# A cross-attention block whose way in and first three blocks are issued in another order

## The chip, the cores and the metric

The kernel runs on one core of a Trainium2 chip. TensorE (PE) multiplies matrices, with weight loads of its own (PEld); VectorE (DVE), ScalarE (ACT) and GpSimd (POOL) do elementwise work; SyncE (SP) issues most transfers. Each engine works through its own instructions in order and waits at semaphores for the others. The metric is device time in microseconds (us), the lower the better. All data are float32.

## The reference

x is (16, 1024, 512), the context (16, 64, 512), the condition (16, 512). Both x and the context are layer-normed and modulated by the condition, then attended with 16 heads of 32, projected, and added to x:

```
def _ada_ln(x, c, W_ss, b_ss):
    h = (x - mu) / jnp.sqrt(var + EPS)
    ss = jax.nn.silu(c) @ W_ss + b_ss
    scale, bias = jnp.split(ss, 2, axis=-1)
    return (1.0 + scale)[:, None, :] * h + bias[:, None, :]
xq  = _ada_ln(x_q,  t_vec, Wss_q,  bss_q)
xkv = _ada_ln(x_kv, t_vec, Wss_kv, bss_kv)
q = (xq @ Wq + bq).reshape(B, Lq, nh, dh)
kv = (xkv @ Wkv + bkv).reshape(B, Lkv, 2, nh, dh)
scores = jnp.einsum('bqhd,bkhd->bhqk', q, kv[:, :, 0]) / sqrt(dh)
attn = softmax(scores)
out = jnp.einsum('bhqk,bkhd->bqhd', attn, kv[:, :, 1]).reshape(B, Lq, H)
return x_q + (out @ Wp + bp)
```

## The kernel before, in words

The 16,384 query rows are 32 blocks of 512 rows (NB = 32, two per batch element). The context is two groups of 512 rows, A (batch elements 0 to 7) and B (8 to 15); all keys and values stay on chip.

The order of all work is written out by hand: the function's last part is a list of calls, and each engine gets its instructions in the order of that list. Nothing reorders them. So what stands in a queue ahead of a waiting instruction matters as much as what it waits for.

The pieces, with their lines:

- Loads: condition (95), context A in four tiles of 256 KB (117), context modulation weights in two loads of 1 MB, scales then shifts (141), key and value weights in four halves (161), block 0 of x (119), query modulation weights (141), query weights (169), context B. They all go through SP's queue. Four small bias rows go through POOL's (150).
- Modulation rows: silu of the condition (L211 to L219), then `scale_shift_rows` (L249): 16 matmuls per half; a copy (L262), a transpose (L268) and an add of the bias (L274) bring them to one column per feature and batch element. `biases` (L227 to L230) transposes the bias rows.
- Context: statistics (`q_stats`, L286 and L287), reciprocal deviation (`rstd_of`, L295 to L310), normalising on ScalarE (`hidden`, L327), 16 transposes on PE (L384), and `modulated` (L402 on ScalarE, L404 on VectorE), which scales each batch element's 64 columns of each feature chunk by its own scale and shift, in an order of columns that is taken apart by 32s.
- Products of 512x512x512 use seven half-sized products instead of eight (`seven`, L503): product n takes a half of the weights, or a sum of halves (`column_sums`, L447 to L450, on POOL), and a half of the features or a sum (`feature_sums`, L467 to L470). Each is 8 matmuls. Results leave through `key_out`, `query_out` (ScalarE, L562, L542), `key_added`, `query_added` (VectorE, L568, L549), `value_out` and `value_added` (L582, L587); `seed` (L515) copies a partial sum into a second bank. For group A the products run 1, 2, 6, 7, 5, 4, 3, keys and values in turns (`context_steps`). Values then move to their place by 16 transfers (`value_move`, L592).
- Block 0 is turned by PE (L412) and scaled (L417). Later blocks are turned by VectorE in 32x32 pieces (`turn`, L351), moved by 16 transfers (`move`, L373; for block 1 half of them through POOL's queue) and scaled in place (`scale_features`, L428).
- Attention for block i: scores in two halves (L627) into two pairs of banks, maxima (L644), copies out (L653), the maximum spread (L675), subtraction on POOL (L688), exponential on ScalarE (L694), totals (L728, L733), a round trip through memory for the reciprocal (L748 to L753), mix with the values (L797), division (L777), projection (`project_seeded`, L842, for block 0; `product`, L927, after), residual add and store.

The list itself (L959 to L1057) first does group A wholly, then block 0's queries in turns with group B's keys, then blocks 1 and 2 up to their turning. The loop from L1060 runs passes i = 0 to 29. A pass does the scores of block i, the queries of block i + 1, the projection of i - 1 and i - 2, and the way in of blocks i + 2 to i + 5. In passes 0 to 2 its projection slots are filled with what is left of group B's keys and values (`slot`) and with the projection of block 0.

Of the kernel before, what the change touches and what calls it, by code (L numbers as in the profile page):

```python
# [20 lines left out]
def cross_attention_block(  # L21
# [116 lines left out]
    def load_scale_shift(name, w, j):  # L138
        pool, tag = SS_HOMES[name, j]
        t = pool.tile([P, NC, H], F32, tag=tag, name=f"wss_{name}_{j}")  # L140
        nc.sync.dma_start(t, w[:, j * H : (j + 1) * H].rearrange("(c p) o -> p c o", p=P))
        w_ss[name, j] = t
# [44 lines left out]
    load_scale_shift("kv", w_ss_kv, 0)  # L187
    load_scale_shift("kv", w_ss_kv, 1)
    for m in range(2):
        for j in range(2):  # L190
            load_context_weights(j, m)
# [14 lines left out]
    BW = 32  # L206
    silu_t = early_tile(P, NC * BW).rearrange("p (c b) -> p c b", c=NC)
    nc.vector.memset(silu_t, 0.0)
    pc = bank("pc")
# [15 lines left out]
    def biases():  # L225
        pb = bank("pb")
        nc.tensor.transpose(pb[:, :NBR], brow, ident[:NBR, :NBR])  # L227
        nc.vector.tensor_copy(bias_t, pb[:, :NBR])
        ones = bias_t[:, : 4 * NC].rearrange("p (n h c) -> p n h c", n=2, h=2)[:, :, 0, :]
        nc.vector.tensor_scalar_add(ones, ones, 1.0)  # L230
# [11 lines left out]
    def scale_shift_rows(name, h):  # L242

        if h == 0:
            pss_tiles[name] = [bank(f"ps{k}_kv") if name == "kv" else spare("ss_q", k) for k in range(2)]
# [18 lines left out]
    def scale_shift(name, off, h, n=1):  # L264
        rows = ssr.pop((name, h))
        pst = pss_tiles[name][1]
        for k in range(n):
            nc.tensor.transpose(  # L268
                pst[:, (h + k) * P : (h + k + 1) * P], rows[:, k * P : (k + 1) * P], ident
            )  # L270
        if h == 0:
            ss[name] = const.tile([P, 2 * NC, BW], F32, name=f"ss_{name}")
        at = slice(h * NC, (h + n) * NC)
        nc.vector.tensor_tensor(  # L274
            ss[name][:, at, :],
            pst[:, h * P : (h + n) * P].rearrange("f (p b) -> f p b", p=n * NC),
            bias_t[:, off + h * NC : off + (h + n) * NC]
            .unsqueeze(2)
            .to_broadcast([P, n * NC, BW]),
            ALU.add,  # L280
        )
# [49 lines left out]
    def hidden(i, ts):  # L331

        for t in ts:
            normalise(x_tiles[i][:, t, :], x_tiles[i][:, t, :], q_rstd[i], t)
# [23 lines left out]
    def features_tile(i):  # L358
        if i in GROUPS:
            pool, tag = (big, "big0") if i == "A" else (qpool, "vb")  # L360
            t = pool.tile([P, 4, NC, NT * 32], F32, tag=tag, name=f"xk_{i}", bufs=1)
# [16 lines left out]
    def turned_features(i, t):  # L378
# [3 lines left out]
        turned[i, t] = spare(f"pxk_{i}_{t // 2}", t % 2)  # L382
# [9 lines left out]
    def modulated(i, j):  # L392
        for c in range(NC):
            for t in range(NT):
                b = GROUPS[i] * PER + 2 * t + j
                at = c * P + j * LKV
                src = turned[i, t][:, at : at + LKV].rearrange("p (z b) -> p z b", z=2)
                dst = xt_tiles[i][:, 2 * j : 2 * j + 2, c, t * 32 : (t + 1) * 32]
                scale = ss["kv"][:, c, b : b + 1]
                shift = ss["kv"][:, NC + c, b : b + 1]  # L400
                if c == NC - 1:
                    nc.scalar.activation(dst, src, AF.Identity, scale=scale, bias=shift)  # L402
                else:
                    nc.vector.tensor_scalar(dst, src, scale, shift, ALU.mult, ALU.add)  # L404

    def turned_queries():

        xt = features_tile(0).rearrange("p g c (t b) -> p c t g b", t=NT)
        pt = [spare(f"pxt_{c // 2}", c % 2) for c in range(NC)]
        for t in range(NT):  # L410
            for c in range(NC):
                nc.tensor.transpose(  # L412
                    pt[c][:, t * P : (t + 1) * P], x_tiles[0][:, t, c * P : (c + 1) * P], ident
                )
        x_tiles.pop(0)
        for c in range(NC):
            nc.scalar.activation(  # L417
                xt[:, c],
                pt[c].rearrange("p (t g b) -> p t g b", t=NT, g=4),
                AF.Identity,  # L420
                scale=ss["q"][:, c, 0:1],
                bias=ss["q"][:, NC + c, 0:1],
            )
# [19 lines left out]
    def column_sums(name, w, tile_, eng):  # L443

        t = wsums[name] = tile_
        tt = eng.tensor_tensor
        tt(t[:, 0], column_half(w, 1, 0), column_half(w, 1, 1), ALU.add)  # L447
        tt(t[:, 1], t[:, 0], column_half(w, 0, 0), ALU.subtract)
        tt(t[:, 2], column_half(w, 0, 0), column_half(w, 1, 0), ALU.subtract)
        tt(t[:, 3], column_half(w, 0, 1), t[:, 1], ALU.subtract)  # L450

    def feature_half(i, k, n):
        return xt_tiles[i][:, 2 * n : 2 * n + 2, k * HC : (k + 1) * HC, :]

    def feature_sums(i, eng=nc.gpsimd):

        if i in GROUPS:
            pool, tag = (big, "big1") if i == "A" else (opool, "ot")
            xsums[i] = pool.tile([P, 4, 2, HC, P], F32, tag=tag, name=f"xk_sums_{i}")
# [5 lines left out]
        tt = eng.tensor_tensor  # L465
        b12 = feature_half(i, 0, 1)
        tt(t[:, 0], feature_half(i, 1, 1), b12, ALU.subtract)  # L467
        tt(b12, b12, feature_half(i, 0, 0), ALU.subtract)
        tt(t[:, 1], feature_half(i, 1, 1), b12, ALU.subtract)
        tt(t[:, 2], feature_half(i, 1, 0), t[:, 1], ALU.subtract)  # L470

    qa = {}
# [14 lines left out]
    def seven(i, name, n, banks):  # L487
# [7 lines left out]
        for m in range(2):  # L495
            for c in range(HC):
                out_ = acc_[:, m * HT : (m + 1) * HT]
                if name == "v":
                    lhsT, rhs = x[:, m, c, :], a[:, c, :]
# [58 lines left out]
    def key_out(i, n):  # L558
        k, m, h = OUTS[n]
        for o in (2 * m, 2 * m + 1):  # L560
            src, dst = places(K_all[i], "k", h, k, o)
            nc.scalar.activation(dst, src, AF.Identity, bias=bk_t[:, o : o + 1])  # L562

    def key_added(i, n):
        k, m, h = ADDS[n]
        for o in (2 * m, 2 * m + 1):
            src, dst = places(K_all[i], "k", h, k, o)
            nc.vector.tensor_tensor(dst, src, dst, ALU.add)  # L568
# [3 lines left out]
    def value_places(i, m, h, k):  # L572
        if i not in stages:
            stages[i] = wpool.tile([P, NC, 4, P], F32, tag="WT", name=f"stage_{i}")
        dst = stages[i][:, 2 * m : 2 * m + 2, 2 * h : 2 * h + 2, :]
        return qa["v", k].rearrange("p (g c f) -> p c g f", g=2, c=2), dst

    def value_out(i, n):
        k, m, h = OUTS[n]
        src, dst = value_places(i, m, h, k)  # L580
        b = b_v_sb.rearrange("p (c f) -> p c f", c=NC)[:, 2 * m : 2 * m + 2, :]
        nc.vector.tensor_tensor(dst, src, b.unsqueeze(2).to_broadcast([P, 2, 2, P]), ALU.add)  # L582
# [6 lines left out]
    def value_move(i, m):  # L589
        for c in (2 * m, 2 * m + 1):  # L590
            for t in range(NT):
                nc.sync.dma_start(  # L592
                    V_all[i][32 * c : 32 * c + 32, 2 * t : 2 * t + 2],
                    stages[i][32 * t : 32 * t + 32, c].rearrange("p (j z) f -> p j z f", j=2),
                )

    def context_steps(i, name, banks):

        ks, vs = (key_out, key_added), (value_out, value_added)
        out_, add_ = ks if name == "k" else vs  # L600
        for n in (1, 2, 6, 7, 5, 4, 3):

            def step(n=n):
                seven(i, name, n, banks)
                if i == "A" and n == 1:
                    out_(i, n)
                elif i == "A" and n == 2:
                    add_(i, n)
                elif n == 1:
                    seed(i, name, banks)  # L610
                elif n in OUTS:
                    out_(i, n)
                else:
                    add_(i, n)

            yield step
# [3 lines left out]
    def scores(i, z, crossed=False):  # L620
# [17 lines left out]
        else:  # L638

            pool, tag = ((hpool, "ht"), (qpool, "xt"))[z]  # L640
        s_sb = pool.tile([P, HPC, TB], F32, tag=tag, name=f"s_{i}_{z}")

        def maximum(e):
            nc.vector.tensor_reduce(  # L644
                m_tiles[i][:, z, 2 * e : 2 * e + 2, :],
                pss[e].rearrange("p r (j a) -> p r j a", a=32),
                AX.X,
                ALU.max,
                apply_transpose=True,
            )  # L650

        def copied(e):
            nc.scalar.copy(s_sb[:, 2 * e : 2 * e + 2, :], pss[e])  # L653


        for step in (
            ((maximum, 0), (copied, 1), (maximum, 1), (copied, 0))
            if crossed
            else ((maximum, 0), (copied, 0), (maximum, 1), (copied, 1))
        ):  # L660
            step[0](step[1])
        s_tiles[i, z] = s_sb
# [176 lines left out]
    def project_seeded(i, t):  # L839
# [10 lines left out]
        projected(i, t)  # L850
# [109 lines left out]
    w_q_sums = qpool.tile([P, 4, HC, HO], F32, tag="wq", name="w_q_sums")  # L960
    biases()
    q_stats("A")
    q_scale("A")
    hidden("A", range(NT))
    turned_features("A", 0)
    scale_shift_rows("kv", 0)
    scale_shift_taken("kv", 0)
    for t in range(1, NT):
        turned_features("A", t)
    scale_shift("kv", 2 * NC, 0)  # L970
    scale_shift_rows("kv", 1)
    scale_shift_taken("kv", 1)
    scale_shift("kv", 2 * NC, 1)
    load_query_weights()
    load_x("B")
    modulated("A", 0)
    modulated("A", 1)
    column_sums("k", w_k_sb, w_k_sums, nc.gpsimd)
    column_sums("v", w_v_sb, wv_sums, nc.gpsimd)
    KA, VA = context_steps("A", "k", (0, 1)), context_steps("A", "v", (2, 3))  # L980
    KB, VB = context_steps("B", "k", (2, 3)), context_steps("B", "v", (2, 3))

    def both_of():
        next(KA)()
        next(VA)()

# [320 lines left out]
```

## Time and profile before

| what | us |
|---|---|
| time before, median of 3 runs | 1046.06 (1042.97 to 1047.47) |
| time of the profiled execution | 1046.14 |
| its span, first to last instruction | 1044.4 |
| PE busy | 1006.6 (96%) |
| PEld busy | 759.3 (73%) |
| DVE busy | 863.4 (83%) |
| ACT busy | 635.5 (61%) |
| POOL busy | 804.5 (77%) |
| mean granted clock of TensorE | 0.998 |

Busy time is the time in which an engine had an instruction under way. "L503" is a line of the kernel. A row "idle before <- X" says how long an engine stood still and what ended that. The chain is the sequence of work that ended last, followed back from the last instruction. HBM read was 79.21 MB and written 34.60 MB, 109 GB/s over the span.

### The profile page before, as it was taken

What the parts mean: (1) busy time and instruction counts of PE and PEld (TensorE: products, weight loads), DVE (VectorE), ACT (ScalarE), POOL (GpSimd) and SP (SyncE); (2) the same over time, 40 slices, a digit from 0 to 9 for tenths busy, and PEclk for the clock granted to TensorE, in tenths of its full rate; (3) what the DMA queues carried; (4) which work ended last, traced back from release to release, by engine and by line L of the source; (5) the groups of instructions that cost most, each with busy time, mean ns of one, the idle gap of its engine ahead of it and who ended that gap; (6) DMA issues with size and microseconds to landing.
All of it is one profiled execution on the core that took longest, in us unless ns stands there. A gap on an engine that the chain in (4) does not pass through costs nothing.

```text
span 1044.4 us, 21138 instructions
## 1 busy us (share of the span) xinstructions
PE 1006.6 (96%) x8041; PEld 759.3 (73%) x8041; DVE 863.4 (83%) x1192; ACT 635.5 (61%) x1011; POOL 804.5 (77%) x518
## 2 busy tenths in 40 slices
PE   3989989999999999999999999999999999999997
PEld 2877656777777877777777777777777777777756
DVE  3766868888888888888888888988889888976794
ACT  2567656667666766666666766766666666665530
POOL 4445678888888898888888889888888889887861
PEclk9999999999999999999999999999999999999999
DMA  9364264554444444544443444554354444345122
GB/s 334 121 163 130 82 187 143 163 164 125 128 150 129 156 145 156 163 135 156 134 151 121 157 154 147 164 163 138 113 162 127 153 150 159 114 123 164 44 83 84
DMA packets 107013, 149.82 MB, mean 143 GB/s; under 512 B 34040, under 2 KB 37136, under 8 KB 106912
## 3 DMA queue, kind: packets, MB, share of 16 engines
q1 hardware_dynamic: 106528, 147.94, 44.4%
q8 instruction: 64, 1.05, 0.4%
q0 software_dynamic: 384, 0.54, 0.2%
q14 instruction: 37, 0.30, 0.1%
HBM read 79.21 MB, written 34.60 MB: 109 GB/s over the span
## 4 chain that ended last, share of the span: by engine, by line
PE 81%; DVE 5%; ACT 3%; POOL 3%; DMA 3%; SPq 2%; issue 1%; DVEq 0%; ACTq 0%; POOLq 0%
PE pq L503 33%; PE pp L927 33%; PE ps L627 6%; PE po L797 6%; SPq L373 2%; POOL s L688 2%; DMA xt<-ht 1%; ACT s L694 1%; DVE m L644 1%; PE pv_A L503 1%; PE pk_A L503 1%; DMA r<-in_x_dram 1%; DVE xk_B L404 1%; DMA w_p_sb<-in_L_xcond_Wp_dram 0%; ACT qt L542 0%
## 5 line engine op out<-in xcount | busy, mean ns | idle before, releaser
L688 POOL TENSOR_TENSOR s<-s,mb 128x2048 f32<-128x2048 f32 x64 | 290.3, 4561 | 138.6 <-DVE mb L675 126.4
L653 ACT COPY s<-ps 128x1024 f32<-128x1024 f32 x128 | 129.6, 1013 | 109.3 <-DVE m L644 69.0
L644 DVE TRANSPOSE_TENSOR_REDUCE m<-ps 128x32 f32<-128x1024 f32 x128 | 150.5, 1213 | 32.2 <-PE ps L627 32.2
L927 PE MATMUL pp<-w_p_sb,ot 128*128 128x256 f32 x720 | 165.4, 379 | 2.3 <-DVE ot L777 1.8
L951 DVE TENSOR_TENSOR r<-pp,r 128x512 f32<-128x512 f32 x203 | 132.0, 671 | 31.3 <-PE pp L927 25.9
L542 ACT ACTIVATE qt<-pq,bias_t 128x256 f32<-128x256 f32 x256 | 105.9, 464 | 78.0 <-PE pq L503 77.8
L927 PEld LDWEIGHTS pp<-w_p_sb,ot 128*128 128x128 f32 x720 | 136.6, 190 | 22.3 <-issue 2.6
L694 ACT ACTIVATE s<-s 128x2048 f32<-128x2048 f32 x64 | 122.4, 1912 | 48.2 <-POOL s L688 48.1
L728 POOL TENSOR_TENSOR sum<-s,s 128x2048 f32<-128x2048 f32 x31 | 140.8, 4541 | 11.7 <-ACT s L694 11.7
L927 PEld LDWEIGHTS pp<-WT,s 128*128 128x128 f32 x480 | 86.5, 189 | 57.0 <-issue 30.2
L503 PE MATMUL pq<-xt_sums,w_q_sums 128*128 128x256 f32 x512 | 123.8, 385 | 0.0
L503 PE MATMUL pq<-xt,w_q_sb 128*128 128x256 f32 x512 | 121.1, 379 | 0.8 <-ACT pq L515 0.8
L503 PEld LDWEIGHTS pq<-xt_sums,w_q_sums 128*128 128x128 f32 x512 | 94.9, 190 | 36.4 <-issue 24.7
L503 PE MATMUL pq<-xt,w_q_sums 128*128 128x256 f32 x512 | 121.0, 379 | 0.0
L927 PE MATMUL pp<-WT,s 128*128 128x256 f32 x480 | 119.3, 391 | 0.2 <-POOL s L906 0.2
L927 PE MATMUL pp<-WT,ot 128*128 128x256 f32 x480 | 113.6, 379 | 0.6 <-POOL ot L903 0.6
L503 PEld LDWEIGHTS pq<-xt,w_q_sb 128*128 128x128 f32 x512 | 97.2, 190 | 15.2 <-ACT pq L515 1.2
L503 PEld LDWEIGHTS pq<-xt,w_q_sums 128*128 128x128 f32 x512 | 97.3, 190 | 13.2
L927 PEld LDWEIGHTS pp<-WT,ot 128*128 128x128 f32 x480 | 91.0, 190 | 14.1 <-POOL ot L903 1.0
L327 ACT ACTIVATE x<-x,rstdq 128x512 f32<-128x512 f32 x128 | 97.0, 809 | 0.3 <-POOL rstdq L304 0.3
L428 ACT ACTIVATE xt<-xt,ss_q 128x512 f32<-128x512 f32 x124 | 93.8, 808 | 2.7 <-DMA xt<-ht 2.6
L286 DVE BATCH_NORM_STATS2 bs<-x 128x6 f32<-128x512 f32 x128 | 87.2, 681 | 0.8 <-DMA x<-in_x_dram 0.8
(179 smaller groups left out, 1491.5 us busy)
## 6 DMA issues: line engine op xcount, KB each, us to landing
x<-in_x_dram SPq DMA_DIRECT2D x32, 1024.0 KB, 5.5
r<-in_x_dram SPq DMA_DIRECT2D x32, 1024.0 KB, 5.1
xt<-ht SPq DMA_DIRECT2D x488, 64.0 KB, 2.0
out_dram<-r SPq DMA_DIRECT2D x58, 512.0 KB, 3.7
out_dram<-r SPq DMA_DIRECT2D x11, 256.0 KB, 2.2
wss_kv<-in_L_xcond_Wss_kv_dram SPq DMA_DIRECT2D x2, 1024.0 KB, 7.8
wss_q<-in_L_xcond_Wss_q_dram SPq DMA_DIRECT2D x2, 1024.0 KB, 12.2
vr<-ltd SPq DMA_DIRECT2D x128, 8.0 KB, 1.6
```

The source lines that it names most:

```text
L286: nc.vector.bn_stats(bs, r)
L327: nc.scalar.activation(dst, src, AF.Identity, bias=rstd[:, 1, j : j + 1], scale=rstd[:, 0, j : j + 1])
L428: nc.scalar.activation(xt[:, :, c, :], xt[:, :, c, :], AF.Identity, scale=ss["q"][:, c, b : b + 1], bias=ss["q"][:, NC + c, b : b + 1],)
L503: nc.tensor.matmul(out_, lhsT=lhsT, rhs=rhs, start=new and m == 0 and c == 0, stop=c == HC - 1, skip_group_check=True,)
L542: nc.scalar.activation(dst, src, AF.Identity, bias=bq_t[:, o : o + 1])
L644: nc.vector.tensor_reduce(m_tiles[i][:, z, 2 * e : 2 * e + 2, :], pss[e].rearrange("p r (j a) -> p r j a", a=32), AX.X, ALU.max, apply_tra ...
L653: nc.scalar.copy(s_sb[:, 2 * e : 2 * e + 2, :], pss[e])
L688: eng.tensor_tensor(s_tiles[i, z], s_tiles[i, z], mb_tiles[i], ALU.subtract)
L694: nc.scalar.activation(p, p, AF.Exp, scale=SCALE)
L728: nc.gpsimd.tensor_tensor(t, s_tiles[i, 0], s_tiles[i, 1], ALU.add)
L927: nc.tensor.matmul(acc[k][:, t * HO : (t + 1) * HO], lhsT=rows[:, c, t * P : (t + 1) * P], rhs=cols[:, c, :], start=n == 2 and t == 0 and ...
L951: nc.vector.tensor_add(r, a, r)
```

## The change

The computation and the sizes stay. What is different:

1. The calls of the way in and of passes 0, 1 and 2 are one flat list of single steps (some 470 calls; each statistic, normalising, turning, sum and copy a call of its own). The loop runs from i = 3, with its conditions for i < 3 removed and otherwise the same calls.
2. 36 transposes of the identity are issued to PE right after the condition's transposes. Nothing reads them.
3. The context's statistics come ahead of the bias copies on VectorE. Tiles 0 and 2 of group A are normalised by VectorE, 1 and 3 by ScalarE.
4. Each load of modulation weights becomes two: the scales and the shifts of one half of the features (512 KB each). So the first pair gives feature chunks 0 and 1 complete, and they can be scaled and multiplied before the second pair is there. Key weights' first half is loaded between the pairs.
5. `modulated` gives even tiles to VectorE and odd tiles to ScalarE, 16 operations each per group (before, 24 and 8), by quarters: feature chunks 0 and 1 or 2 and 3, rows 0 to 255 or 256 to 511.
6. Context features stay in the order of their rows. Keys and values come out in that order; `key_added` is one instruction instead of two; `value_move` takes rows of 128 elements instead of 512.
7. Seeds, outs and adds are calls apart from their products; in the list group A runs 1, 2, 7, 6, 5, 4, 3, and block 0's products stand among the last of group A and the first of group B. Group B's values stand among block 1's and 2's queries.

```
+        for h in range(2):
+            at = h * H + j * (H // 2)
+            nc.sync.dma_start(
+                t[:, :, h * (H // 2) : (h + 1) * (H // 2)],
+                w[:, at : at + H // 2].rearrange("(c p) o -> p c o", p=P),
+            )
...
     load_scale_shift("kv", w_ss_kv, 0)
+    load_context_weights(0, 0)
     load_scale_shift("kv", w_ss_kv, 1)
...
+            row, rstd = x_tiles[i][:, t, :], q_rstd[i]
+            if i == "A" and t % 2 == 0:
+                nc.vector.tensor_scalar(
+                    row, row, rstd[:, 0, t : t + 1], rstd[:, 1, t : t + 1], ALU.mult, ALU.add
+                )
...
-    def modulated(i, j):
+    def modulated(i, k, n, eng):
+        t = 2 * n if eng is nc.vector else 2 * n + 1
+        for c in (2 * k, 2 * k + 1):
+            for j in range(2):
...
+                src = turned[i, t][:, at : at + LKV]
+                dst = xt_tiles[i][:, c, t * P + j * LKV : t * P + (j + 1) * LKV]
...
     def key_added(i, n):
         k, m, h = ADDS[n]
-        for o in (2 * m, 2 * m + 1):
-            src, dst = places(K_all[i], "k", h, k, o)
-            nc.vector.tensor_tensor(dst, src, dst, ALU.add)
+        src = qa["k", k].rearrange("p (o n) -> p o n", o=2)
+        dst = K_all[i][:, 2 * m : 2 * m + 2, h * HT : (h + 1) * HT]
+        nc.vector.tensor_tensor(dst, src, dst, ALU.add)
...
+    warm = bank("warm", 1)
+    for _ in range(WARM):
+        nc.tensor.transpose(warm[:, :P], ident, ident)
+    q_stats("A", (0,))
...
+    q_scale("A")
+    hidden("A", (3,))
+    hidden("A", (1,))
+    scale_shift_rows("kv", 0)
     biases()
-    q_stats("A")
-    q_scale("A")
-    hidden("A", range(NT))
+    hidden("A", (0,))
+    column_sums("k", w_k_sb, w_k_sums, (2,))
     turned_features("A", 0)
...
+    modulated("A", 0, 0, nc.vector)
     scale_shift_rows("kv", 1)
+    modulated("A", 0, 1, nc.scalar)
+    context_product("A", "k", 1)
...
+    hidden("B", (3,))
+    turned_features("B", 0)
+    modulated("B", 0, 0, nc.vector)
+    turned_features("B", 1)
+    context_product("A", "v", 3)
...
+    query_product(0, 1)
+    modulated("B", 0, 0, nc.scalar)
+    query_seed(0)
...
+    query_product(0, 7)
+    context_product("B", "k", 2)
...
+    score_products(0, 0)
+    context_product("B", "k", 4)
+    maximum(0, 0, 0)
...
+    query_product(1, 6)
+    move(2)
+    copied(0, 1, 0)
+    query_product(1, 7)
+    context_out("B", "v", 1)
+    maxima(0)
...
-    for i in range(NB - 2):
+    for i in range(3, NB - 2):
```

## The prediction

> **What bounds the kernel now.** I read first the page's busy times, then the chain of work that ended last, then PE's busy time stretch by stretch, and last the waits and the timeline of the stretches with gaps.
>
> ```profile
> PE 1006.6 (96%) x8041; PEld 759.3 (73%) x8041; DVE 863.4 (83%) x1192; ACT 635.5 (61%) x1011; POOL 804.5 (77%) x518
> ...
> PE 81%; DVE 5%; ACT 3%; POOL 3%; DMA 3%; SPq 2%; issue 1%; DVEq 0%; ACTq 0%; POOLq 0%
> ```
>
> TensorE is busy for 96% of the span and carries 81% of the chain. Two lines of the chain in order of time, the second product of a softmax block, show the loop's period:
>
> ```profile
> 190.65 2.28 PE po L797 x62
> ...
> 219.84 2.34 PE po L797 x63
> ```
>
> They lie 29.19 us apart. That loop is not edited: from its pass i = 3 on, the list of calls is the same in both kernels. So I cut the span at events of the trace: third pair of context products starts (32.48), first query product (56.07), scores of block 0 (79.58), scores of block 3 (177.68, where pass i = 3 begins). Columns: stretch, its length, then busy us of PE, PEld, DVE, ACT, POOL, granted clock, DMA share, GB/s.
>
> ```profile
> 0.00:32.48 32.48, 14.96 (x120) 11.87 (x120) 15.02 (x52) 8.35 (x18) 12.87 (x18) 1.00 0.94 332
> 32.48:56.07 23.59, 23.36 (x178) 20.37 (x179) 16.24 (x39) 13.85 (x33) 12.39 (x20) 1.00 0.23 71
> 56.07:79.58 23.51, 20.31 (x89) 16.11 (x87) 15.72 (x45) 15.17 (x37) 9.88 (x16) 1.00 0.64 169
> 79.58:177.68 98.10, 88.89 (x624) 61.22 (x624) 71.55 (x102) 62.58 (x102) 67.35 (x41) 0.98 0.47 141
> 177.68:1044.40 866.72, 859.08 (x7033) 649.77 (x7032) 744.87 (x957) 535.51 (x823) 702.04 (x424) 1.00 0.43 138
> ```
>
> Length less the first busy number is PE's idle time: 17.52, 0.23, 3.20, 9.21 and 7.64 us. The change touches the first four, 30.2 us of idle time in all. No order can win much more than that, and the way in has a floor set by its loads.
>
> **The way in (0 to 32.48).** The timeline shows what is late (start, length, engine):
>
> ```profile
> 9.58 0.69 DVE L286 BATCH_NORM_STATS2 bs<-x_A 128x6 f32<-128x512 f32 x1
> ...
> 15.21 1.12 PE L384 MATMUL pxk_A<-ident,x_A 128*128 128x128 f32 x4 [5.97 <-ACT x_A L327]
> 16.25 1.93 PE L249 MATMUL ps_kv<-wss_kv,early 128*32 128x128 f32 x32
> 18.12 2.35 PE L384 MATMUL pxk_A<-ident,x_A 128*128 128x128 f32 x12
> ...
> 20.50 1.08 PE L249 MATMUL ps_kv<-wss_kv,early 128*32 128x128 f32 x32
> ...
> 22.69 3.12 DVE L404 TENSOR_SCALAR xk_A<-pxk_A,ss_kv 128x64 f32<-128x64 f32 x12
> ```
>
> The statistics of the context sit on VectorE behind the bias copies, and those behind four small loads (PE waited 5.8 us for the last, until 8.97). The context's rows were there earlier: the last of four issues ended by 3.06 and took at most 4.4 us, so 7.5 at the latest. The new list puts the statistics first. VectorE is free of the silu at 4.64; the four take 3.28 (9.58 to 12.86), so they end between 7.9 and 8.4; I take 8.0. The inverse root takes 1.48 as now (12.86 to 14.34): 9.5 instead of 14.34.
>
> The modulation rows now need both feature halves, together the 1 MB that the first load was: issued at 3.06, landed 6.7 us later, 9.8. Ahead of them stand 36 idle transposes, from 3.2. Their price is bounded by two rows: 0.28 us each (four in 1.12, above) ends them at 13.3; 0.12 each (the 16 of the first query block in 1.91, at 42.21) ends them at 7.5. I take the row between, 2.35 / 12 = 0.20, so 10.4. What they buy is in the same rows: the sixteen transposes cost 3.47 where sixteen later ones cost 1.91, and the first rows 1.93 where the second cost 1.08, together 2.4 us. The granted clock reads 1.00 throughout, so these durations, not that column, show a slow start. The Trainium skill (TensorE: Matmul & The Clock Gate, Part 1, "What's actually happening") says that the array runs at half rate until some 3.4 us of activity and falls back after an idle window of that length; by it, an estimate, 12 transposes at 0.28 and 24 at 0.12 end at 9.5, and the stage would gain 0.9 us more than I take.
>
> Then step by step: rows 10.4 + 1.08 = 11.5; bias transpose 0.27, two copies 0.35: 12.1; VectorE normalises tile 0, copies the rows (0.29) and normalises tile 2. Normalising there has no row; a 128x512 add took 0.69, a 128x64 scaling 0.26; I take 0.69, the same size: 13.8. ScalarE does tiles 3 and 1 meanwhile (0.73 each, from 9.5). Tile 2's transposes 0.48, the rows' transpose 0.27, the add 0.29: 14.9. Scaling of the first two feature chunks can start there, against 22.69. Each engine has 4 operations a quarter (VectorE 0.26, ScalarE 0.32 each): first quarter 16.2; first key product to 18.0; the second rows (second 1 MB; 3.5 MiB at the stage's pace, about 14) are copied inside this; their transpose and add end at 18.6. The other two quarters take ScalarE 8 x 0.32: 21.2. Key and value products 1 and 2 follow by 23.6, the first feature sum (0.69) by 22.0. The third pair starts at **23.7 instead of 32.48: 8.8 us**. With idle transposes at 0.28, or the context landing late, 6.5; with both cheap ends, 10.5.
>
> Pool's column sums wait for the same loads (first at 17.07 now; its third operation, needed by product 7 of the values, ends by 21) and are no bound. Against the halves speaks a rule: the Trainium skill (DMA: Bandwidth & Descriptors, "Measured (HBM→SBUF, ...)") advises batches of 1 MiB and more. Here loads of 256 and 512 KB already share the queue in this stretch at 332 GB/s and a DMA share of 0.94; if smaller batches cost a tenth of the pace, the 1 MB lands 0.7 later, under the idle transposes.
>
> **Context group A (to 56.07).** PE is already full (0.23 idle). Loads in the new order: block 0 and both query weights by about 27, context B by 30, query weights by 33 (cumulative bytes at the stage's pace); statistics of block 0 on VectorE from 27.2, its rstd through Pool's queue by 32.6, normalised by 35.7 (four at 0.73), transposed at 36.8. Cover is about 1 us. I take 0, bounds -1.5 to +0.2: query weights' first sum stands in Pool's queue ahead of context B's rstd.
>
> **Block 0's queries (to 79.58).** The waits of PE after 56 us (total, times, longest):
>
> ```profile
> PE pq L503 <- ACT qt L542: 4.6, 3, 2.1
> PE ps L627 <- ACT s L653: 2.9, 2, 1.9
> PE pk_B L503 <- ACT pk_B L515: 1.5, 1, 1.5
> ...
> PE pp L927 <- DVE ot L777: 1.0, 1, 1.0
> ```
>
> Now block 0's products wait for group B's scaling (8 operations on ScalarE behind 24 on VectorE) and its seed. The list scales B in 16 and 16, by halves, between query products, and puts key product 5 ahead of the scores. I take 2.0 of 3.2, bounds 0 to 3.5.
>
> **Blocks 0 to 2 (98.10).** 9.21 idle, and two key products at 87.73 took 5.24 instead of 2 x 1.73, behind a 1.88 us wait: 1.8 more. The 4.6 us row is product 5 of each query block waiting for a bank that ScalarE empties after an exponential (1.91). In the list, in blocks 0 and 2's passes the copies stand ahead of that exponential or the next products ahead of the copy (8 us of projection before product 4): gone. Context B's value products now stand between. Kept: the second scores wait for the first's copies (2.9; one product of 1.73 lies between in block 1, less than the 2.2 of two copies). I take 6.5 of 11.0. Bounds +12.5 (tails of stalls too) and -3, three blocks with one more copy wait of 1.0 each.
>
> **Hidden or small.** Each value move now has 512 B runs instead of 2 KB, same bytes; block 0's mix needs group A's 50 us later; uncovered they would cost their issue time, 11 us for 16. Key additions go from two of 0.38 to one of 0.69: nothing.
>
> **Sum.** 8.8 + 0 + 2.0 + 6.5 = 17.3. The profiled execution took 1046.14 (span 1044.4, 1.7 around it; the median 1046.06 is the same): **1028.8 us**. Sum of lower bounds +2, of upper 26.7.
>
> **Rivals.**
> 1. Only the way in is won: block 1's features come through a transfer that took from 69.54 to 80 now (8 issues on SP in 6.5, 8 on Pool), behind the load of block 3, as in the new list. If it and ScalarE's new queue (context halves mixed with queries) take back stages three and four, the gain is 8.8 less up to 3: 1037 to 1041. For: PE moves ahead, transfers don't shrink. Against: their inputs are ready earlier by the same 9 us. 22%.
> 2. No measurable change (0.5%, 5.2 us, is about what a measurement of this kernel tells): way in 6.5, and lower bounds after. 1041 to 1051. That the idle transposes do not do what they say belongs here, priced 2.4. 7%.
> 3. Slower: the loop inherits another phase. Pool works 702 of 867 us there and VectorE 745; each pass has Pool's subtraction (9.06) between the scores and the exponential. If pass 3 starts with ScalarE and Pool later relative to PE and this persists, each of 27 passes pays. From 0.85 us a pass (23 us) it is slower by over 0.5%: 1052 and more. Against: PE has 99% of the loop, so a late engine catches up. 9%.
>
> The forecast's case (gain 13 to 26) has 62%. The range 1021 to 1041 takes in rival 1 and leaves out rivals 2 and 3 and a little at the fast end. Faster by over 0.5%: 62 + 22 = 84%; within: 7%; slower: 9%.
>
> **What would show it.** First statistics near 4.7 and first scaling near 15; sixteen transposes in about 2 us; the third pair near 24; first query product near 47; scores of block 0 near 69 and of block 3 near 160; period still 29.19. Wrong if scores of block 3 come after 172, or if the period grows.

## The result, and the profile after

The changed kernel takes 1031.61 us (median; 1030.86 to 1033.82), the kernel before, beside it, 1045.21 (1042.97 to 1047.47). The ratio is 0.9873, 95% interval 0.9846 to 0.9901. The forecast was 1028.8 in a range of 1021 to 1041. The profiled execution took 1030.86 (span 1029.1) against 1046.14: 15.3 us gained, where the steps had summed to 17.3. By the medians it is 13.6: the profiled execution is the fastest of the changed kernel's four, and the one before lies 0.9 above its median.

The page's busy times and chain after, as read before:

```profile
PE 1009.3 (98%) x8077; PEld 763.4 (74%) x8077; DVE 860.9 (84%) x1174; ACT 638.6 (62%) x1025; POOL 805.9 (78%) x518
...
PE 81%; SPq 6%; DMA 5%; DVE 4%; ACT 1%; issue 1%; POOL 1%; DVEq 0%; ACTq 0%; POOLq 0%
```

TensorE's work is the same but for the 36 idle transposes. In the chain SP's queue has gone from 2% to 6%: remember that line. The stretches between the same five events (same columns as before: length, busy us of PE, PEld, DVE, ACT, POOL, clock, DMA share, GB/s):

```profile
0.00:22.58 22.58, 18.38 (x155) 16.06 (x156) 13.99 (x46) 9.29 (x24) 8.00 (x14) 1.00 0.96 313
22.58:45.90 23.32, 22.87 (x175) 19.93 (x175) 15.60 (x33) 14.10 (x32) 12.35 (x17) 1.00 0.63 218
45.90:67.64 21.74, 21.52 (x102) 18.48 (x100) 17.53 (x46) 17.87 (x47) 17.09 (x26) 1.00 0.72 209
67.64:162.62 94.98, 87.34 (x618) 59.31 (x617) 69.27 (x95) 62.25 (x103) 68.53 (x42) 0.98 0.45 127
162.62:1029.10 866.48, 859.17 (x7032) 649.60 (x7032) 744.50 (x957) 535.10 (x822) 700.00 (x422) 1.00 0.44 140
```

Shorter by 9.9, 0.3, 1.8, 3.1 and 0.2 us. One key product (1.73 us) has moved from the fourth stretch into the third, so blocks 0 to 2 have in truth gained only 3.1 - 1.7 = 1.4 by their order. TensorE's idle time there is 7.64 us, 1.6 less than the 9.21 of before. The loop's period is what it was:

```profile
206.71 2.28 PE po L826 x62
235.90 2.28 PE po L826 x62
```

29.19 us. (The last stretch hides three small things: its first pass, block 3's, takes 31.12, 1.9 over the period, with a wait of TensorE of 1.3; passes of the loop before were 1.2 longer than 29.19 together, one of them 30.14; and the last blocks are 0.95 shorter.) The way in, in order of time:

```profile
3.13 5.83 PE L991 MATMUL warm<-ident 128*128 128x128 f32 x36
4.55 0.68 DVE L294 BATCH_NORM_STATS2 bs<-x_A 128x6 f32<-128x512 f32 x1
12.11 1.53 PE L400 MATMUL pxk_A<-ident,x_A 128*128 128x128 f32 x12 [0.93 <-DVE x_A L344]
14.11 1.10 DVE L419 TENSOR_SCALAR xk_A<-pxk_A,ss_kv 128x64 f32<-128x64 f32 x4
22.58 1.94 PE L539 MATMUL pk_A<-xk_sums_A,w_k_sums 128*128 128x256 f32 x8
```

Statistics at 4.55 instead of 9.58, the twelve transposes in 1.53 instead of 2.35, the first scaling at 14.11 instead of 22.69. What TensorE waits for between 45 and 163 us (total, times, longest):

```profile
PE pp L871 <- ACT pp L866: 2.9, 1, 2.9
PE ps L658 <- ACT s L684: 2.3, 3, 1.5
PE pq L539 <- DVE qt L585: 1.6, 1, 1.6
```

The 4.6 us row (query products waiting for a bank) is gone, as forecast. In its place TensorE has a row that it did not have before: 2.9 us for the seed of a projection. Follow it back through the timeline, one engine after the other:

```profile
104.97 10.65 SPq L387 DMA_DIRECT2D xt<-ht  x16
115.73 1.10 SPq L126 DMA_DIRECT2D r<-in_x_dram  x2
126.71 0.69 DVE L882 TENSOR_TENSOR r<-pp,r 128x512 f32<-128x512 f32 x1 [5.12 <-DMA r<-in_x_dram]
127.44 0.59 ACT L866 COPY pp<-b_p_sb 128x512 f32<-128x512 f32 x1 [6.30 <-DVE r L882]
128.08 5.40 PE L871 MATMUL pp<-w_p_sb,ot 128*128 128x512 f32 x8 [2.92 <-ACT pp L866]
```

Block 0's residual (x a second time, 1 MB) is called for in SP's queue behind the 16 transfers that move block 3's features, 10.65 us of issues. It is issued at 116.4 and lands at 126.6. VectorE's residual add waits for it, the bank of the next seed for the add, TensorE for the seed. And then the eight matmuls take 5.40 instead of the 3.5 that 16 of them in 7.03 make: behind the idle time TensorE has lost its pace too. That is 2.9 + 1.9 us at one place.

The late load is older than the change. In the kernel before, the move's 16 issues took 11.01 us (from 119.11), block 0's residual was called for at 130.23 and landed at 135.71, and the wait for it reached TensorE by another way:

```profile
135.80 0.69 DVE L854 TENSOR_TENSOR r<-pp,r 128x512 f32<-128x512 f32 x1 [6.19 <-DMA r<-in_x_dram]
136.53 0.59 ACT L837 COPY pp<-b_p_sb 128x512 f32<-128x512 f32 x1 [3.14 <-DVE r L854]
141.22 1.97 PE L503 MATMUL pq<-xt_sums,w_q_sb 128*128 128x256 f32 x8 [2.08 <-ACT qt L542]
```

ScalarE's copy waited for the add, the exponential (138.44) and the query result (140.25) stood behind the copy. GpSimd's subtraction, which that exponential needs, was done by 133.6. So 2.08 of the 4.6 us row was this load.

The new list also exchanged two loads: before, block 0's residual was called for first and block 1's behind it; now block 1's (another 1 MB) stands ahead. Block 0's took 5.5 us from issue to landing before, and 10.2 now. An estimate from these numbers: issued first, at 115.73, and landing 5.5 to 5.7 later (5.7 is what it took in experiment 6, which has the old order), it would be there at about 121.3, just when VectorE begins to wait (121.6). No run exchanged these two loads alone.

### The profile page after: what moved, and what is told of

Same layout as the page of the kernel before. It is cut to its first block, busy times and chain, and to the rows that moved or that the text cites. A ratio compares the mean times of both kernels' runs of the same rounds, so it can differ in the third digit from the quotient of the medians.

```text
span 1029.1 us, 21212 instructions
## 1 busy us (share of the span) xinstructions
PE 1009.3 (98%) x8077; PEld 763.4 (74%) x8077; DVE 860.9 (84%) x1174; ACT 638.6 (62%) x1025; POOL 805.9 (78%) x518
## 4 chain that ended last, share of the span: by engine, by line
PE 81%; SPq 6%; DMA 5%; DVE 4%; ACT 1%; issue 1%; POOL 1%; DVEq 0%; ACTq 0%; POOLq 0%
PE pp L955 34%; PE pq L539 33%; PE po L826 6%; PE ps L658 6%; SPq L387 4%; DMA ltd<-lt 1%; SPq L631 1%; PE pk_A L539 1%; PE pv_A L539 1%; DMA xt<-ht 1%; DMA r<-in_x_dram 1%; DVE ht L365 1%; DVE lt L762 1%; DMA wss_kv<-in_L_xcond_Wss_kv_dram 1%; DMA x<-in_x_dram 1%
## 5 line engine op out<-in xcount | busy, mean ns | idle before, releaser
L539 PE MATMUL pq<-xt,w_q_sb 128*128 128x256 f32 x512 | 121.6, 380 | 0.3 <-ACT pq L551 0.2
L539 PEld LDWEIGHTS pq<-xt_sums,w_q_sums 128*128 128x128 f32 x512 | 94.9, 190 | 36.5 <-issue 24.8
L955 PEld LDWEIGHTS pp<-WT,ot 128*128 128x128 f32 x480 | 91.0, 190 | 14.1 <-POOL ot L931 1.0
L498 POOL TENSOR_TENSOR xt_sums<-xt 128x512 f32<-128x512 f32 x64 | 81.4, 1272 | 14.2 <-ACT xt L447 7.3
```

The lines of the kernel that those rows point to most:

```text
L498: eng.tensor_tensor(dst, a, b, ALU.subtract)
L539: nc.tensor.matmul(out_, lhsT=lhsT, rhs=rhs, start=new and m == 0 and c == 0, stop=c == HC - 1, skip_group_check=True,)
L955: nc.tensor.matmul(acc[k][:, t * HO : (t + 1) * HO], lhsT=rows[:, c, t * P : (t + 1) * P], rhs=cols[:, c, :], start=n == 2 and t == 0 and ...
```

## The experiments

Theory at the start: the way in won what was forecast, and blocks 0 to 2 lost part of their gain to TensorE's new wait, whose cause is the place of one load in SP's queue. Rivals: the transfers themselves (not their order) are the bound there; or the worked-out order of blocks 0 to 2 is worth nothing.

**1. The residual earlier.**

```
     load_x(5)
+    load_residual(0)
     turn(3, (3,))
...
-    load_residual(1)
     q_scale(4)
     context_product("B", "v", 3)
-    load_residual(0)
+    load_residual(1)
```

> The load of block 0's residual is issued ahead of block 3's move instead of behind its 16 issues; block 1's residual load takes its old place. Theory: in the changed kernel VectorE stands 5.1 us at 126.7 for that load, PE stands 2.9 behind it at 128.1 and then runs its next projection at 5.4 us instead of 3.6; with the load early all 4.7 us go, block 2's scores start near 128.7 instead of 133.4, time about 1027. Rival: SyncE's queue of issues is the bound there, and block 3's move or the value move only comes late in its place: block 2's scores at 131 or later, time 1030 to 1033.

1030.34 us (ratio to before 0.986, 0.9844 to 0.9877). My theory fell in this form: block 2's scores came at 134.97 (133.41 in the changed kernel). The wait at 128 was gone, but the reciprocals' way to memory (32 KB) took 6.61 instead of 3.37 us beside the 1 MB load, the move of block 3's features began 5 us later, and TensorE waited again, a little earlier, with the slow pace behind it:

```profile
126.23 2.62 PE L539 MATMUL pq<-xt_sums,w_q_sb 128*128 128x256 f32 x8 [2.80 <-ACT qt L578]
```

**2. No idle transposes** (`WARM = 0`).

> The 36 idle transposes are left out, nothing else. Theory: the first modulation rows and the transposes of the context run at the slow pace of the kernel before (1.93 for the rows instead of 1.1, 0.20 to 0.28 a transpose instead of 0.12): the third pair of products starts 1.5 to 2.4 us later than 22.6, and the time is 1033 to 1034. Rival: the loads and the normalising set the pace there and PE has room, third pair within 0.4 us, time unchanged at 1031 to 1032.

1033.52 us (0.9902, 0.9874 to 0.993). The first twelve transposes show what the 36 buy:

```profile
13.44 2.82 PE L400 MATMUL pxk_A<-ident,x_A 128*128 128x128 f32 x12 [0.93 <-DVE x_A L344]
```

0.235 us each instead of 0.128; the rows before them were slow as well. The third pair is at 25.38, 2.8 later than in the changed kernel's profile and 1.7 later than the mean of its ways in (experiment 7 has them). The end is 1.9 us later by the medians: as expected, though the two intervals overlap, and the third pair is a little later than the theory's 24.1 to 25.0.

**3. Bias transposes ahead of the rows** (`biases()` and `scale_shift_rows("kv", 0)` exchanged).

> PE transposes the bias rows ahead of the context's modulation rows instead of behind them. Theory: in the changed kernel VectorE waits for that transpose (until 11.2) before it may normalise tile 0, so a modulation weight load at 9.9 holds the context's features too; with the change tile 0 is normalised from about 9.6, the first scaling starts near 12 instead of 14.1, the second pair of weights (14.5) then holds, third pair near 21 instead of 22.6, and 1.5 us reach the end: 1030. Rival: the way in is won but context B (used at 31.9) and the query weights (34.5) land when they did, so the first query product stays at 45.9 and the time at 1031 to 1032.

1031.2 us (0.9867, 0.985 to 0.9883). First scaling 0.8 earlier (13.29), third pair not earlier (23.55), end the same. The rival had the end right. The second pair of modulation weights, waited for until 14.4, is what comes next in this run (the second rows go on at 14.44, the second value product at 17.38 as in the changed kernel's profile), so the earlier start bought nothing. A difference under a microsecond would be lost in the spread of unedited ways in (experiment 7).

**4. Statistics behind the bias copies**, as before.

> The bias transposes and copies stand ahead of the context's statistics again, as in the kernel before; the rest as changed. Theory: statistics start near 9.6 instead of 4.6, the deviation is there at 14.3 instead of 9.5, but VectorE's part of the normalising only started at 11.5, so the scaling starts at about 16.8 instead of 14.1 and the third pair near 25 instead of 22.6: time 1034. Rival: the whole 4.8 us come back, third pair near 27.4, time 1036.4.

1035.68 us (0.991, 0.9893 to 0.9926). Between the two: TensorE, already warm, waits 3.85 us and is slow again.

```profile
15.60 2.94 PE L400 MATMUL pxk_A<-ident,x_A 128*128 128x128 f32 x12 [3.85 <-DVE x_A L344]
```

The third pair is at 28.58, 4.9 later than the mean way in, and block 2's scores (137.72) and the end are 4 later. The theory (25, 1034) was too low, the rival (27.4, 1036.4) nearer: at the third pair more than the 4.8 came back, since the pace was lost too. Of the parts of the way in that were taken out, the order of the statistics is the largest, and a gap of 3.85 us behind the idle transposes was enough to lose what they buy.

**5. Scales of all features, then shifts**, as before.

> The changed kernel, with the context's modulation weights loaded as before: the scales of all features, then the shifts of all, and only then the first key and value weights. Theory (the loads of the way in run back to back at 0.96 of the transfer engines, so the order decides): the first half of the features has scale and shift only when about 2 MB more has landed, at 11.4 to 12.8 us instead of 9.9; the row products, the bias transposes behind them and the first scaling are later by that, the second half's rows are earlier, so the third pair of products starts 1 to 2 us later (23.5 to 24.6) and the end is 0 to 1.5 us later: 1031 to 1033. Rival (halves are what lets the scaling start): the third pair 3 us or more later, the end 1034 or more.

1034.43 us (1032.31 to 1038.56; 0.9897, 0.9863 to 0.9931). The rows waited until 11.60 instead of 9.94 and the first scaling came at 15.77, 1.7 later, inside the theory's bounds. The third pair came at 23.96, as the theory had it, but the spread of unedited ways in (experiment 7) covers that. The end was where the rival had it (1034 or more), 2.8 us later by the medians; the intervals overlap, so its size stays open.

**6. The old order for blocks 0 to 2.** The changed kernel's list up to block 0's scores, then the loop of before from i = 0.

> The changed kernel up to block 0's first score products, then the loop of the kernel before for blocks 0 to 2 in place of the worked-out list. Theory (nearly all the gain is the way in; the worked-out order of blocks 0 to 2 is worth only the 1.4 us by which that stage shortened): block 0's scores at 67 to 68.7 as in the changed kernel, block 3's about 1 to 2 us later than its 162.6, end 1032 to 1034. Rival (the old order with the work 12 us earlier meets transfers that are not yet done, and the list is what carries the gain on): block 3's scores at 167 or later, end 1036 to 1041.

1037.16 us (0.9917, 0.9899 to 0.9936). The theory fell: the list of blocks 0 to 2 is worth about 5 us (5.6 by the medians, 0.0044 x 1045 = 4.6 by the ratios, whose intervals just touch), not the 1.4 of the stage sum. Block 0's scores were at 69.52 and block 3's at 170.86: 101.3 us, 3.2 more than the 98.1 of the kernel before, with a key product (1.73) less to do. Started 10 us earlier, the old order loses 5 us: 2.5 before block 1's scores (with the product counted), 2.4 between these and block 2's. TensorE's waits from 50 to 170 us show where:

```profile
PE pq L539 <- ACT qt L578: 4.4, 2, 3.2
PE ps L658 <- ACT s L684: 2.5, 2, 1.3
PE pv_B L539 <- ACT K_B L599: 2.0, 1, 2.0
```

The bank row of before (4.6) is back at 4.4; its 3.2 us stand behind VectorE's wait of 7.39 for block 0's residual, also at 127 us, the same load behind the same move. It landed only 8.5 us earlier than in the kernel before, where the work ran 10 earlier: that part of the loss is a transfer. The other part hardly is one: ScalarE waited 0.9 us before it scaled block 1's features (0.4 before). The wait of 2.0 for `K_B`, with a slow product behind it (3.49), stands at 81.7, where the key product that is now ahead of the scores no longer covers ScalarE's copies. So the stage compared with its own past hid what the list does: on this way in, some 5 us are lost without it. How much of the 2.5 comes only from joining the old loop to the new way in is not shown.

**7. The division 24 to 8** of the group's scaling, as before (`c % 2 == 0` of the odd tiles to VectorE).

> The changed kernel with the scaling of the two context groups divided between VectorE and ScalarE as before, 24 pieces to 8 instead of 16 to 16. Theory (in the changed way in VectorE has 0.27 us a piece and also the statistics, sums and copies there, so the pieces it takes over come one after the other): 8 pieces more at 0.27 us are 2.2 us on VectorE, of which the products' waits show 0.6 to 1.5; third pair 0.6 to 1.5 us later than the 22.6 to 24.4 seen so far, the end 0 to 1 us later, 1031 to 1033. Rival (ScalarE at 0.31 us a piece is the slower of the two and its share sets the end): the third pair earlier and the end at 1030 to 1031.

1033.88 us (1032.86 to 1036.99; 0.9913, 0.9893 to 0.9934). The third pair is at 24.24, no later than in other runs; the loss is at group B, where VectorE takes the pieces beside its other work: block 0's scores 70.59, 1.3 later than in a run with the same third pair. At the end it is 2.3 us by the medians, more than expected, with intervals that overlap a little.

This run made me look at the third pair in all eight runs whose way in is the changed kernel's: 22.6, 22.8, 23.4, 23.5, 24.1, 24.2, 24.4, 24.8, mean 23.7. The first feature sum in two of them, the changed kernel's, then that of experiment 8:

```profile
20.89 0.91 DVE L498 TENSOR_TENSOR xk_sums_A<-xk_A 128x512 f32<-128x512 f32 x1
```

```profile
21.57 1.80 DVE L498 TENSOR_TENSOR xk_sums_A<-xk_A 128x512 f32<-128x512 f32 x1
```

The values' bias row, loaded last of the weights, lands up to 1.2 us too late (VectorE waits 0.25 for it in the first, 0.91 in the second), and the feature sum beside GpSimd's column sums takes 0.68 to 1.81. The changed kernel's profile has the best of these ways in.

**8. The residual right behind the reciprocals**, ahead of the move.

```
     inverse_rows(0)
+    load_residual(0)
     move(3)
...
-    load_residual(0)
```

> The changed kernel with block 0's residual load issued right behind the loads of the reciprocals and ahead of the 16 issues that move block 3's features; nothing else moved. Theory (the 5.12 us wait of VectorE at 121.6 is a place in SyncE's queue: the load waits behind 16 issues of 0.66 us): the load is issued at 105 instead of 116 and lands at 109 to 114; the wait on it, the late seed copy and the 2.92 us wait of TensorE at 128 go, and with no idle time the projection there takes 3.6 instead of 5.4 us; block 2's scores at 129 to 131 instead of 133.4, the end 1027 to 1029. Rival (the transfers themselves are the limit there, as in the run with the load still earlier): 1 MB shares the engines with block 3's features, whose scaling comes 2 to 5 us later, and the wait only moves to the query products of block 2: block 2's scores at 133 or later, end 1030 to 1031.

1029.33 us (0.9846, 0.9826 to 0.9865). From block 0's scores to block 2's 62.86 instead of 65.77 us: 2.9 gained, the wait of 5.12 and the slow projection gone. A wait of 1.50 at 125 remains:

```profile
125.01 1.97 PE L539 MATMUL pq<-xt_sums,w_q_sb 128*128 128x256 f32 x8 [1.50 <-ACT qt L578]
...
128.54 3.60 PE L871 MATMUL pp<-w_p_sb,ot 128*128 128x512 f32 x8
```

So the place in the queue was the cause; too early, ahead of the reciprocals (experiment 1), gained nothing at block 2. Both edits take the load out from behind the 16 issues and from behind block 1's residual, so they do not tell the two apart. At the end it is 2.3 us by the medians, with intervals that overlap; the reading rests on the trace.

**9. And one value product of group B between block 1's two score products.**

> As the run with block 0's residual behind the reciprocals, and the last value product of context B put between the two score products of block 1 as well, where TensorE waits 1.46 us for the copies of the first scores. Theory (the stall at 101.6 us is a lack of work between the two, and lies on the path): both stalls go, block 2's scores 1 to 1.5 us earlier than without this edit, the end 1026 to 1028. Rival (what follows is held by SyncE's queue and block 3's features, not by TensorE): the stall is found again as a wait before 130 us, and the end is that of the other run within 0.5 us.

1029.3 us (0.9845, 0.9824 to 0.9865): the rival. The wait of 1.46 at 101 was gone and came back at 122:

```profile
106.39 12.15 SPq L387 DMA_DIRECT2D xt<-ht  x16
...
120.04 0.81 ACT L447 ACTIVATE xt<-xt,ss_q 128x512 f32<-128x512 f32 x1 [3.50 <-DMA xt<-ht]
...
124.22 3.64 PE L539 MATMUL pq<-xt_sums,w_q_sb 128*128 128x256 f32 x8 [2.06 <-ACT qt L578]
```

Block 3's move ends at 118.5, ScalarE waits for it, and a query result and an exponential stand behind it in ScalarE's queue.

**10. Experiment 9 with block 3's move on two queues** (`move(3, two=True)`: 8 of 16 issues on GpSimd's).

> The run with the residual behind the reciprocals and the value product between (1029.3), with every second one of the 16 issues that move block 3's features given to GpSimd's queue in place of SyncE's, as block 1's are. Theory (the move takes 12.15 us because SyncE issues its 16 transfers one after the other, 0.7 us each): on two queues it takes 6 to 8 us, block 3's first scaling comes at 114 to 116 instead of 120.0 and the exponential and the query results behind it with it; the 2.06 us wait of TensorE at 122 and the slow product after it (3.64 instead of 1.89) go; end 1026 to 1028. Rival (GpSimd is itself on the way there: it subtracts the maxima from 109 to 118, and its issues come in between): the subtraction ends 2 to 5 us later, the exponential and the query results behind it too, and the end is 1029 to 1033.

1027.89 us (0.9843, 0.9829 to 0.9858).

```profile
106.25 7.29 SPq L387 DMA_DIRECT2D xt<-ht  x8
...
115.66 0.80 ACT L447 ACTIVATE xt<-xt,ss_q 128x512 f32<-128x512 f32 x1
...
121.20 1.89 PE L539 MATMUL pq<-xt_sums,w_q_sb 128*128 128x256 f32 x8
```

In the trace the theory held: the move's part on SP 7.29 us, the scaling at 115.66 without a wait, the product on time and at full pace. GpSimd's subtraction stayed at 9.05 us, so the rival fell. Block 2's scores are 60.4 us behind block 0's. The ratio does not differ from that of experiment 9, although the profiled execution (span 1024.1) does.

**11. Experiment 9 with ScalarE's and VectorE's order changed**: query result and exponential ahead of the scaling that waits.

> The run with the residual behind the reciprocals and the value product between (1029.3), with ScalarE's order changed: block 2's query result (2,7) and the second exponential of block 1 ahead of the scaling of block 3's features, for which ScalarE waits 3.50 us; VectorE's statistics of block 5 ahead of the turn that waits 4.01 us. Theory (nothing of what TensorE waits for at 122 needs block 3's features, it only stands behind them): query result at 116 to 118 instead of 123.3, no wait and no slow product at 122 to 128, the exponential at 118.4 instead of 120.8; block 2's scores at about 129.3 where the way in is the same, 3.5 earlier; end 1026 to 1027.5. Rival (block 3's features then come late for its own sums and first query product): the stall is found again at block 3's first query products, 134 to 150 us, and the end is 1028.5 to 1030.

1029.37 us (0.9854, 0.9837 to 0.9871). Block 2's scores are 60.67 behind block 0's, as good as in experiment 10, and TensorE did not wait between 105 and 130 us. But 1.58 us came back at 147.7 (VectorE had waited 2.05 for the reciprocals) and 2.25 at 157.1, where VectorE waited 5.22 for block 4's move in the same way. The rival had the end right.

**12. All of it, and block 4's move on two queues too.**

> All of the edits that moved the stall together: block 0's residual behind the reciprocals, the value product between, the query result ahead of the scaling, block 3's features on two queues, and block 4's features on two queues as well, for which VectorE waits 4.41 us at 145 in the run with block 3's on two (1027.9). Theory (the issues in one queue, one after the other, are what holds blocks 1 and 2): TensorE runs from 105 to 152 without a wait over 0.7 us; the waits of VectorE for the features of block 4 (4.41) and of TensorE behind it (0.98) go; scores of block 3 at about 156 where the third pair of products starts at 22.8, the end 1025 to 1027, 3 to 5 us under the changed kernel. Rival (what is saved before the steady loop is given back in its first pass, whose period is set by what the blocks before left over, as when the residual alone was moved and block 3's pass took 30.0 us in place of 29.2): scores of block 3 earlier, the pass after it longer, the end 1028 to 1030.

1026.38 us (1024.14 to 1026.87; 0.9809, 0.979 to 0.9828), faster than the changed kernel: the two intervals do not meet. What each of the edits adds at the end is not shown: experiments 8 to 11 agree within their intervals. TensorE's longest waits between 45 and 163 us are now 1.3 (a projection's bank, at 156.9), 0.8 and 0.6.

VectorE's wait of 4.41 us for block 4's features is gone; 0.48 is left at that turning. This way in was the latest of the eight (24.75), and still block 3's scores came at 158.96, 89.1 behind block 0's; in the changed kernel 95.0, before 98.1. Block 3's pass then took 29.95, so part of the rival is there too (0.8 us).

## Why the prediction was right, and where it was not

- **Way in, 8.8.** Right: 9.9 in the profile, 8.7 by the mean of eight ways in (32.48 - 23.7; of the kernel before there is one trace). The steps in order, forecast and measured: statistics end 8.0 and 8.1; inverse root 9.5 and 9.5; rows 11.5 and 11.0; first scaling 14.9 and 14.1. The idle transposes took 0.16 us each (0.20 assumed) and the normalising on VectorE 0.54 (0.69 assumed); against that the first feature sum took up to 1.81 where 0.69 stood in the sum, and the values' bias row, which was not in the sum, came up to 1.2 late. That the mean meets the forecast to 0.1 is luck: such errors cancel. Experiments 2 and 4 show the parts against the mean way in: 1.7 for the warm array, 4.9 for the statistics with it.
- **Halves of the weights.** They bring 0.8 to 1.7 us at the first scaling (15.77 in the one run of experiment 5, 14.0 to 14.9 in the unedited ways in); at the third pair no gain is shown. The 1 MB pair's smaller loads cost nothing that the DMA share (0.96) shows.
- **Group A, 0.** Right: 23.32 for 23.59.
- **Block 0's queries, 2.0.** Right in sum (1.8), and better than that by the key product that is now in the stretch: TensorE idles there 0.22 us of 21.74. Of the 1.2 us of waits that I kept, 0.2 remain.
- **Blocks 0 to 2, 6.5.** This is the step that failed: 3.1 came, 1.4 without the moved product, and the first pass after them gave 1.9 back. The 4.6 us row went, as forecast, but I had read its cause only in part: I put it down to a bank emptied after an exponential, and did not ask why that exponential came late at 138.44. Its longest wait, 2.08, goes back to block 0's residual in SP's queue, as the kernel before shows (VectorE's wait of 6.19). The list did away with the row and left the load behind the 16 issues, 0.67 us each, and put block 1's residual ahead of it as well. So the wait came out at another place: 2.92, with 1.9 of slow pace (5.40 for 3.5), about as much as the 1.8 of slow pace that I took as won. Experiment 8 shows that it is the place in the queue; experiments 9 to 11 show the next moves in that queue behind it.
- **What the step compared with.** I took the old order's 98.1 us as what would happen without the list. Experiment 6 shows 101.3 and a product less: on the new way in the old order loses 5 us. Rival 1 had such a loss, with the range 1037 to 1041, and the old order on the new way in takes 1037.2. But it named the transfer of block 1's features; experiment 6 shows the residual of block 0 for about half of the loss, and only 0.5 us more of waiting before block 1's features are scaled. So a loss of rival 1's size is what the list prevents; the mechanism is mostly another.
- **The sum.** 15.3 in the profiles for 17.3 is also errors that cancel: blocks 0 to 2 gave 3.4 too little, the way in 1.1 and group A 0.3 more than forecast, in the best way in of eight.
- **Loop.** Right: the period is 29.19 and rival 3 did not come. A way in that was 1.0 later (block 0's scores 67.64, and 68.65 in experiment 3) was not seen at block 2's (133.41, 133.44), nor was one 3 us later in experiment 7 (70.59; 133.17). But 1.4 later in experiment 5 came out as 2.4 (69.06; 135.82). That blocks 1 and 2 wait for transfers anyway fits the first two and is not shown as a rule.

## What to carry to other kernels

Follow a wait back past the engine that ends it, as far as the queue that issues a transfer: the row that you remove may only have been the place where a late load showed. When work moves earlier, list for each such queue what now stands ahead of each load, with issue time times count and the bytes of the loads. Don't price an order by the stretch it had: run the old order at the new starting point. And when one stall goes, look for it one queue further on before counting it as won.

## What the runs showed of the hardware

- **The pace of TensorE after a wait.** Waits of 2.65, 2.80, 2.92, 3.23 and 3.85 us were each followed by slow matmuls. From 1.9 to 2.6 us it went both ways: after 1.88, 2.03 and 2.06 eight products took 3.46, 3.49 and 3.64 (normal 1.89), after 2.05, 2.08 and 2.25 they took 1.97 to 1.99; eight matmuls of a projection took 5.40 after 2.39 (experiment 5) and 3.70 after 2.56 (experiment 2). The Trainium skill (TensorE: Matmul & The Clock Gate, Part 1) gives half rate until a busy window of some 3.4 us, back after an idle window of that length, with windows that run freely. The runs agree with the two rates (0.235 and 0.128 us) and with a result that varies at one wait length, but shorter waits than a window sufficed here. The granted clock in tens of us shows it only roughly (0.97 and 0.85 around the 5.40; 0.69 in the 4 us from 128).
- **A small round trip beside a large load.** The 32 KB of the reciprocals took 1.5 us to land by the median of the run, 2.6 to 4.9 at about 100 us, some 2.5 us behind a 1 MB load, and 6.6 behind two.
- **A sum on VectorE beside one on GpSimd.** The same 128x512 sum took 0.68 to 1.81 us while GpSimd ran column sums. The Trainium skill (SBUF — State Buffer, Who interferes with whom) has the two share one port pair that an instruction holds to its end; the runs fit that. In the kernel before, GpSimd stood idle at these sums and each took 0.69. And either engine can be the one that waits: beside VectorE's 1.80 (experiment 8) GpSimd's two sums took 2.49, as the two before them with no such sum beside; beside VectorE's 0.68 (experiment 1) they took 3.04.
- **GpSimd as a second queue.** Eight of 16 issues moved there brought the first scaling behind the move 4.4 us forward and cost its own work nothing visible: the subtraction took 9.05 us as before.
